# A block product inside a fast block product: seven smaller products for one, in fifteen of sixteen stages of an expert network

## The chip, the cores and the metric

The kernel runs on one core of a Trainium2 chip. A core has TensorE (matrix products, in the profile PE for the products and PEld for loading their stationary operand), VectorE (DVE), ScalarE (ACT), GpSimd (POOL), which here mostly issues gathers and scatters, and SyncE (SP), which issues most other transfers. Each takes its instructions in order. On-chip memory is SBUF, 128 partitions; TensorE writes its sums into the eight banks of PSUM, from which VectorE and ScalarE read them. The metric is the device time in microseconds of one execution; a kernel's time is the median of several.

## The reference, cut to what matters

```python
styles = w @ (affine_w * gain).T + affine_b
y = einsum('blc,oc->blo', x * styles[:, None, :], weight) * dcoefs[:, None, :]
y = clip(y + bias, -256, 256)                       # (8, 512, 512): 4096 tokens of 512

scores = softmax(y.reshape(4096, 512) @ Wr)         # 8 experts
G, idx = top_k(scores.T, 1024)                      # each expert takes its 1024 best tokens
X_in = y.reshape(4096, 512)[idx]                    # (8, 1024, 512)
h = gelu(einsum('ekd,edh->ekh', X_in, W1) + b1)     # (8, 1024, 2048)
X_e = einsum('ekh,ehd->ekd', h, W2) + b2            # (8, 1024, 512)
out = x + zeros.at[idx].add(G[..., None] * X_e)
```

All is float32. The two products of the experts are nearly all of the arithmetic.

## The kernel before, in words

A first part, to about 165 us of the profile, computes y and the scores and chooses the first expert's tokens. Then come eight experts, each in two passes p over half of the 2048 hidden columns (the loop at lines 1205 to 1228). A pass is a hidden stage (the first product, 1024 tokens x 512 x 1024 hidden columns, with Gelu, into the tile H) and an output stage (the second, whose rows are scaled by the gain and added to the result in memory by GpSimd's scatter, line 1156). So there are 16 hidden and 16 output stages.

Each stage splits its matrices into 2x2 blocks and uses a fast block product (Winograd's form of Strassen's): seven block products for eight, paid for by sums of blocks. For the hidden stage the token blocks are called 11, 12, 21, 22 with sums s1 to s4 (`left_sums`, line 927), and the weight blocks (i, j) with sums t1 to t4 (`weight_sum_steps`, line 183). A stage has four units, one for each 128 columns of a block: `hidden_unit` (line 1031) and `out_unit` (line 1102). A unit is seven functions p1 to p7, one block product each (two matmuls of 128x512 in a hidden unit, four of 128x256 in an output unit):

- p1 starts bank a, p6, p5 and p3 add further products to it; after each, ScalarE reads the bank, either as a copy ("snap", lines 1059 and 1123) or as the last result.
- p2 uses bank b: token block 12 by weight block (1, 0). VectorE adds p1's copy (line 1072), and ScalarE's Gelu makes the first block of H.
- p7 and p4 share bank c; VectorE adds copies to it (lines 1087 and 1096).

PSUM has two banks a, one b, two c, two for transposes (`ps_t`) and one small. `in_turns` (line 999) interleaves a unit with the last two products, p3 and p4, of the one before. It also releases side work behind a unit's mark (the sum of p2): at the third unit of a hidden stage the four sums of second weights, at the third unit of an output stage those of the next first weights; in an expert's second pass `fetch` for the next expert at the first hidden unit and `prepare` at the first output unit.

`fetch` calls `indices` (line 834): VectorE builds a one-hot tile `oh` (line 849) and `val`, TensorE turns them into token indices (line 855), and `gather` (line 904) fetches 8 x 128 token rows by GpSimd (line 913) into row buffers, of which there are four, writes them back to memory by SP (line 917) and reads them in a layout for VectorE's transposes (line 919). `prepare` (line 946) transposes on VectorE (line 952) and forms s1 to s4. In the first hidden stage the side work is `route_others` (line 737), the choice of tokens for the other seven experts: a long exchange between VectorE and small products of TensorE, which ends in the first output stage.

What sets the order: in the first part, TensorE's instructions are held in the written order by `in_order` (line 77). The experts' products (`product`, line 1025) are not: they are placed by the scheduling layer from the order of the calls and the dependencies, and `tc.issue_after` keeps side work behind its mark. Tiles of one tag share buffers: a new one waits until the old one's readers are done. H has one buffer, as has every weight block.

SP's loads stand in order: `load_w1` for the next pass is called after the hidden stage, `load_w2` after the output stage (lines 1222 and 1228), each four transfers of 512 KB that wait for their blocks.

Of the kernel before, what the change touches and what calls it, by code (L numbers as in the profile page):

```python
# [20 lines left out]
P = 128  # L21
# [4 lines left out]
def tile_modulated_expert_choice_ffn(  # L26
# [76 lines left out]
    pk = const.tile([P, P], I32, name="pk")  # L103
    nc.gpsimd.iota(pk, pattern=[[0, P]], base=0, channel_multiplier=1)
    pm = const.tile([P, P], I32, name="pm")
    nc.gpsimd.iota(pm, pattern=[[1, P]], base=0, channel_multiplier=0)
    ek = const.tile([P, P], I32, name="ek")
    nc.vector.tensor_scalar(ek, pk, E - 1, None, op0=ALU.bitwise_and)
    em = const.tile([P, P], I32, name="em")
    nc.vector.tensor_scalar(em, pm, E - 1, None, op0=ALU.bitwise_and)  # L110
    same = const.tile([P, P], BF16, name="same")
    nc.vector.tensor_tensor(same, ek, em, ALU.is_equal)
    ahead = const.tile([P, P], BF16, name="ahead")
    nc.vector.tensor_tensor(ahead, pk, pm, ALU.is_lt)
    nc.vector.tensor_mul(ahead, ahead, same)
# [49 lines left out]
    QD = D // 2  # L165
    w1_blocks, w2_blocks = {}, {}
# [28 lines left out]
    def weight_sums(kind, blk, name):  # L195
        for _ in weight_sum_steps(kind, blk, name):
            pass

# [538 lines left out]
    def route_others():  # L737

        ST = rt.tile([P, 2, P], F32, tag="ST", name="ST")
# [15 lines left out]
        mark = rt.tile([P, 2, P], F32, tag="run", name="mark")  # L755
# [18 lines left out]
        def ranks(mask, name):  # L774

            run = rt.tile([P, 2, P], F32, tag="run", name=f"run_{name}")
# [12 lines left out]
            nc.vector.tensor_copy(off, ps)  # L789
            return run, off  # L790


        sel = rt.tile([P, 2, P], F32, name="sel")
# [3 lines left out]
        eq = rt.tile([P, 2, P], F32, name="eq")  # L797
# [22 lines left out]
        pos_i = rt.tile([P, NT, E], I32, tag="ST", name="pos_i")  # L820
        nc.vector.tensor_scalar(pos_i.rearrange("p t e -> p (t e)"),
                                ps.rearrange("p h m -> p (h m)"), -1.0, None, op0=ALU.add)
        part = rt.tile([P, NT, E], I32, tag="part", name="part")
# [3 lines left out]
        part2 = rt.tile([P, NT, E], I32, tag="part", name="part2")  # L827
        nc.vector.tensor_scalar(part2, pos_i, 7, None, op0=ALU.logical_shift_right)
        hi = rt.tile([P, NT, E], BF16, name="hi")
        nc.vector.tensor_copy(hi, part2)  # L830
# [3 lines left out]
    def indices(e):  # L834
# [14 lines left out]
        nc.vector.tensor_tensor(  # L849
            oh, lo.unsqueeze(2).to_broadcast([P, NT, P]),  # L850
            iota_lo.unsqueeze(1).to_broadcast([P, NT, P]), ALU.is_equal,
        )
# [51 lines left out]
    def gather(e, i):  # L904
# [40 lines left out]

    def prepare(e):
# [9 lines left out]
        left_sums(xT[0, 0], xT[0, 1], xT[1, 0], xT[1, 1], s)  # L956

# [41 lines left out]
    def in_turns(units, between):  # L999
# [5 lines left out]
        for n in range(len(units)):  # L1005
# [15 lines left out]
            held = unit[5:]  # L1021
        for f in held:
            f()

    def product(ps, lefts, rights, start):
        n = len(lefts)
        for k in range(n):
            nc.tensor.matmul(ps, lefts[k], rights[k], start=(start and k == 0), stop=(k == n - 1),  # L1028
                             skip_group_check=True)

    def hidden_unit(e, p, u, H, early=False):
# [12 lines left out]

        def begin(cols):
# [11 lines left out]
        def snap(n):  # L1057
            t = sp.tile([P, HALF], F32, tag=f"snap{n}", name=f"snap{n}_{name}")
# [41 lines left out]
        return (begin, unit) if early else unit  # L1100

    def out_unit(e, p, v, H, b2_sb):
# [7 lines left out]
             for n in ("s1", "s2", "s3", "s4")}  # L1110
# [94 lines left out]
    for e in range(E):  # L1205
        b2_sb = fx.tile([P, D], F32, tag="b2", name=f"b2_{e}")
        nc.sync.dma_start(b2_sb, b2[e, :].partition_broadcast(P))
        for p in range(NP):
# [60 lines left out]
```

## Time and profile before

| | us |
|---|---|
| median of three runs | 1750.95 (1750.62 to 1751.68) |
| the profiled execution's own time | 1745.7 |
| its span, first to last instruction | 1743.9 |
| TensorE products busy | 1718.0 (99% of the span) |
| weight loads busy | 1136.2 (65%) |
| VectorE busy | 830.8 (48%) |
| ScalarE busy | 480.2 (28%) |
| granted TensorE clock, mean | 0.996 |

A row of instructions names line and engine, what is written from what, shape, and count. A float32 matmul stands as two passes, each with its own weight load, so a hidden unit's block product shows as x4 and an output unit's as x8. Matmul passes overlap in the pipeline: the time that counts is from the start of one to the start of the next. Tiles are named ps_a_h, ps_b_h, ps_c_h for the banks in a hidden stage, ps_a_o and so on in an output stage, hs_o for the sums of H's blocks, xs for those of the tokens, w_t for those of the weights, snap for ScalarE's copies.

### The profile page before, as it was taken

To read this page: it belongs to the slowest core of one execution; us is meant where nothing else is said; L and a number is where in the kernel's file an instruction comes from. 1 tells how busy PE (TensorE), PEld (TensorE's weight loads), DVE (VectorE), ACT (ScalarE), POOL (GpSimd) and SP (SyncE) were. 2 spreads that over 40 slices of the span, in tenths; PEclk is the share of its full clock that TensorE was granted. 3 is DMA by queue.
4 is the path that set the end of the run, shared out by engine and by line. 5 is a ranking of instruction groups with operands and counts; after the bars stand their busy time and mean duration, and the time that the engine had idled before them with its cause. 6 is when DMAs were issued, how large, how long until landed. Compare 5 with 4: busy or idle time off the path is not lost.

```text
span 1743.9 us, 17415 instructions
## 1 busy us (share of the span) xinstructions
PE 1718.0 (99%) x6646; PEld 1136.2 (65%) x6646; DVE 830.8 (48%) x1467; ACT 480.2 (28%) x845; POOL 293.5 (17%) x238
## 2 busy tenths in 40 slices
PE   9998999999999999999999999999999999999997
PEld 5775475665748485766758485766758484756656
DVE  5885884524535254624535254614444254614341
ACT  3543312223131322222231313222231313222231
POOL 0112013020212013110312012110302012110202
PEclk9999999999999999999999999999999999999999
DMA  9625527441574237442574237432564137332403
GB/s 207 171 50 197 192 55 179 106 85 49 97 201 73 48 61 183 90 85 55 100 191 85 49 63 176 90 79 55 112 179 90 46 64 186 75 79 61 85 0 49
DMA packets 143252, 178.59 MB, mean 102 GB/s; under 512 B 16825, under 2 KB 92857, under 8 KB 143041
## 3 DMA queue, kind: packets, MB, share of 16 engines
q1 hardware_dynamic: 118240, 115.19, 24.4%
q0 software_dynamic: 24912, 62.27, 21.0%
q8 instruction: 52, 0.85, 0.2%
q14 instruction: 32, 0.25, 0.0%
q10 hardware_dynamic: 16, 0.02, 0.0%
HBM read 120.46 MB, written 65.37 MB: 107 GB/s over the span
## 4 chain that ended last, share of the span: by engine, by line
PE 93%; DVE 4%; ACT 1%; issue 1%; DMA 1%; POOL 0%; POOLq 0%; DVEq 0%; ACTq 0%
PE ps_a_o L1028 25%; PE ps_a_h L1028 23%; PE ps_c_o L1028 12%; PE ps_c_h L1028 12%; PE ps_b_o L1028 6%; PE ps_b_h L1028 6%; PE ps_ya L81 2%; PE ps_yc L81 1%; DVE oh L849 1%; PE ps_y L81 1%; ACT xmT L500 1%; DVE mark L760 1%; PE ps_yt L727 1%; PE ps_a_h_a L1028 0%; PE ps_yb L81 0%
## 5 line engine op out<-in xcount | busy, mean ns | idle before, releaser
L1156 POOL DMA_INDIRECT out<-o_o,idx x128 | 213.2, 1666 | 1246.7 <-DVE o_o L1153 497.0
L1028 PE MATMUL ps_a_o<-w_t,hs_o 128*128 128x256 f32 x1024 | 243.3, 380 | 1.2
L1028 PE MATMUL ps_a_h<-xs,w_t 128*128 128x512 f32 x496 | 233.4, 592 | 0.0
L1028 PEld LDWEIGHTS ps_a_o<-w_t,hs_o 128*128 128x128 f32 x1024 | 192.3, 190 | 33.7 <-issue 7.2
L1028 PEld LDWEIGHTS ps_a_h<-xs,w_t 128*128 128x128 f32 x496 | 94.1, 190 | 119.1 <-issue 118.5
L1059 ACT COPY snap_h<-ps_a_h 128x512 f32<-128x512 f32 x186 | 108.2, 582 | 230.0 <-PE ps_a_h L1028 227.0
L1123 ACT ACTIVATE snap_o<-ps_a_o,gain 128x256 f32<-128x256 f32 x128 | 60.6, 474 | 346.7 <-PE ps_a_o L1028 346.7
L1087 DVE TENSOR_TENSOR snap_h<-snap_h,ps_c_h 128x512 f32<-128x512 f32 x64 | 43.9, 687 | 217.5 <-ACT snap_h L1059 217.5
L1072 DVE TENSOR_TENSOR ps_b_h<-ps_b_h,snap_h 128x512 f32<-128x512 f32 x62 | 43.4, 699 | 202.6 <-PE ps_b_h L1028 202.6
L1028 PE MATMUL ps_c_o<-w,hs_o 128*128 128x256 f32 x512 | 124.2, 380 | 0.0
L1028 PE MATMUL ps_a_o<-w,H 128*128 128x256 f32 x512 | 124.0, 379 | 0.0
L1028 PE MATMUL ps_a_o<-w,hs_o 128*128 128x256 f32 x512 | 121.6, 380 | 0.0
L1028 PE MATMUL ps_b_o<-w,H 128*128 128x256 f32 x512 | 121.1, 379 | 0.0
L1028 PE MATMUL ps_a_h<-xT,w 128*128 128x512 f32 x248 | 120.7, 594 | 0.0
L1028 PE MATMUL ps_c_h<-xs,w 128*128 128x512 f32 x256 | 120.5, 593 | 0.0
L1028 PE MATMUL ps_c_h<-xT,w_t 128*128 128x512 f32 x256 | 120.5, 593 | 0.0
L1028 PE MATMUL ps_c_o<-w_t,H 128*128 128x256 f32 x504 | 119.1, 379 | 0.0
L1028 PE MATMUL ps_a_h<-xs,w 128*128 128x512 f32 x248 | 118.2, 599 | 0.0
L1028 PE MATMUL ps_b_h<-xT,w 128*128 128x512 f32 x248 | 116.8, 593 | 0.0
L1028 PEld LDWEIGHTS ps_a_o<-w,H 128*128 128x128 f32 x512 | 97.1, 190 | 27.0 <-issue 15.5
L1028 PEld LDWEIGHTS ps_a_o<-w,hs_o 128*128 128x128 f32 x512 | 95.9, 190 | 21.8 <-ACT snap_o L1123 9.2
L1028 PEld LDWEIGHTS ps_c_o<-w,hs_o 128*128 128x128 f32 x512 | 97.0, 190 | 13.9 <-issue 0.6
(277 smaller groups left out, 1983.8 us busy)
## 6 DMA issues: line engine op xcount, KB each, us to landing
w<-in_w SPq DMA_DIRECT2D x120, 512.0 KB, 4.1
rows<-row SPq DMA_DIRECT2D x56, 260.0 KB, 3.9
xg<-rows SPq DMA_DIRECT2D x56, 256.0 KB, 6.4
x<-in_x SPq DMA_DIRECT2D x28, 256.0 KB, 8.4
y_dram<-ytok SPq DMA_DIRECT2D x5, 1024.0 KB, 4.3
w<-in_w SPq DMA_DIRECT2D x32, 128.0 KB, 3.5
y_dram<-ytok POOLq DMA_DIRECT2D x12, 256.0 KB, 5.0
b<-in_b SPq DMA_DIRECT2D x8, 256.0 KB, 4.2
```

The lines of the kernel that those rows point to most:

```text
L81: behind[engine] = make()
L500: nc.scalar.mul(t, t, styles[1][:, j, b : b + 1])
L727: nc.tensor.transpose(ps[:, o * P : (o + 1) * P], yT[:, o, t * P : (t + 1) * P], ident)
L760: nc.vector.tensor_scalar(mark, ST, cand[:, c + 1 : c + 2].bitcast(F32), None, op0=ALU.is_ge, op1=ALU.add, accum_out=cnt[:, c : c + 1])
L849: nc.vector.tensor_tensor(oh, lo.unsqueeze(2).to_broadcast([P, NT, P]), iota_lo.unsqueeze(1).to_broadcast([P, NT, P]), ALU.is_equal,)
L1028: nc.tensor.matmul(ps, lefts[k], rights[k], start=(start and k == 0), stop=(k == n - 1), skip_group_check=True)
L1059: nc.scalar.copy(t, st["a"])
L1072: added = nc.vector.tensor_add(st["b"], st["b"], st["s1"])
L1087: nc.vector.tensor_add(st["u4"], st["u4"], st["c"])
L1123: nc.scalar.mul(t, st["a"], scale)
L1156: nc.gpsimd.indirect_dma_start(out=last_rows[g] if e == E - 1 else out_rows, out_offset=bass.IndirectOffsetOnAxis(ap=idx[:, e, g : g + 1], ...
```

## The change: what it does

In 15 of the 16 hidden stages (all but the first) the product p2, block 12 by block (1, 0), over all four units, is itself done by the same seven-product form on its own 2x2 blocks: two groups r of seven products, each a single matmul of 128x256 (`second_level`). Its parts go to a tile q in SBUF; the banks are b and the two of `ps_t`. `hidden_stage` takes the place of `in_turns` there: units in the order 0, 2, 1, 3, the small products put behind the large ones by a plan, and `finish(u)` takes unit u's share of q to the sum with p1's copy and the Gelu. The sums that this needs are `second_sums` (tokens) and the four additions in `weight_sums`. An output stage's last p3 and p4 are handed on (`keep`, `held`) and issued inside the next hidden stage, and the second weights' load is called there, behind them (`then`).

To make room in SBUF: the first constants are in a pool that is given back; routing works in the buffers of gathered rows, whose number goes from four to three; the output units' sum s1 overwrites H's block; the token sums of the second level use the place of block 21. The copy of p1 has three buffers instead of two. The one-hot tile is built in four parts.

Left out of the diff below are the renamed routing tiles, the constants' pool, and lines that only hand on arguments.

```diff
 def weight_sums(kind, blk, name):
...
+        if kind == "w1":
+            b = {(k, j): blk[1, 0][:, k, j * Q : (j + 1) * Q] for k in range(2) for j in range(2)}
+            t = wpool.tile([P, 3, Q], F32, tag="w1_l2", name=f"w1_l2_{name}")
+            t1, t2, t4 = [t[:, n, :] for n in range(3)]
+            nc.vector.tensor_add(t1, b[0, 0], b[0, 1])
+            nc.vector.tensor_add(t2, t1, b[1, 1])
+            nc.vector.tensor_add(t4, t2, b[1, 0])
+            nc.vector.tensor_add(b[0, 1], b[0, 1], b[1, 1])
+            blk["l2"] = {**b, "t1": t1, "t2": t2, "t3": b[0, 1], "t4": t4}
...
-        nc.vector.tensor_tensor(
-            oh, lo.unsqueeze(2).to_broadcast([P, NT, P]),
-            iota_lo.unsqueeze(1).to_broadcast([P, NT, P]), ALU.is_equal,
-        )
+        for n in range(4):
+            here = slice(n * NT // 4, (n + 1) * NT // 4)
+            nc.vector.tensor_tensor(
+                oh[:, here, :], lo[:, here].unsqueeze(2).to_broadcast([P, NT // 4, P]),
+                iota_lo.unsqueeze(1).to_broadcast([P, NT // 4, P]), ALU.is_equal,
+            )
...
-            to = gp.tile([P, YW], F32, tag="row", name=f"row_{e}_{g}", bufs=4)
+            to = gp.tile([P, YW], F32, tag="row", name=f"row_{e}_{g}", bufs=3)
...
+    def second_sums(e):
+        s = tokens[e][0]
+        a = {(i, k): s["12"][:, k, i * Q : (i + 1) * Q] for i in range(2) for k in range(2)}
+        t = fx.tile([P, 4, Q], F32, tag="xT10", name=f"x2_{e}")
+        s2 = {f"s{n + 1}": t[:, n, :] for n in range(4)}
+        left_sums(a[0, 0], a[0, 1], a[1, 0], a[1, 1], s2)
+        tokens[e][0]["l2"] = {**s2, "11": a[0, 0], "12": a[0, 1], "22": a[1, 1]}
...
         left_sums(xT[0, 0], xT[0, 1], xT[1, 0], xT[1, 1], s)
+        second_sums(e)
...
+    def second_level(e, p, r):
+        s, blk = tokens[e][0]["l2"], w1_blocks[e, p]["l2"]
+        name = f"{e}_{p}_{r}"
+        q = sp.tile([P, 2, HALF], F32, tag="q", name=f"q_{name}", bufs=1)
+        out = {(i, j): q[:, j, i * Q : (i + 1) * Q] for i in range(2) for j in range(2)}
+        st = {}
+        def mm(tag, left, right, start):
+            if start:
+                st[tag] = (bank("b", f"q{name}", 1) if tag == "b" else
+                           ps_t.tile([P, HALF], F32, tag="t", name=f"ps_q{tag}_{name}"))[:, 0:Q]
+            product(st[tag], [blk[right][:, r * P : (r + 1) * P]], [s[left]], start)
+        def snap(n, scale=1.0):
+            t = sp.tile([P, Q], F32, tag=f"q{n}", name=f"q{n}_{name}", bufs=1)
+            nc.scalar.mul(t, st["a"], scale)
+            return t
+        def p1():
+            mm("a", "11", (0, 0), True)
+            st["s1"] = snap(1)
+        def p2():
+            mm("b", "12", (1, 0), True)
+            return nc.vector.tensor_add(out[0, 0], st["b"], st["s1"])
+        def p6():
+            mm("a", "s2", "t2", False)
+            st["u2"] = snap(2)
+        def p7():
+            mm("c", "s3", "t3", True)
+        def p5():
+            mm("a", "s1", "t1", False)
+            st["u4"] = snap(4, -1.0)
+            nc.vector.tensor_sub(out[1, 1], st["u4"], st["c"])
+        def p3():
+            mm("a", "s4", (1, 1), False)
+            nc.scalar.mul(out[0, 1], st["a"], -1.0)
+        def p4():
+            mm("c", "22", "t4", False)
+            nc.vector.tensor_add(out[1, 0], st["c"], st["u2"])
+        return [p1, p2, p6, p7, p5, p3, p4], q
+
+    def hidden_stage(e, p, H, between, held, then):
+        unit = {u: hidden_unit(e, p, u, H) for u in range(U)}
+        steps, results = zip(*[second_level(e, p, r) for r in range(2)])
+        g = [iter(x) for x in steps]
+        def finish(u):
+            return unit[u][1](results[u % 2][:, u // 2, :])
+        def second(r, n=1):
+            for _ in range(n):
+                done = next(g[r])()
+            return done
+        mark = None
+        plan = [
+            (0, [partial(second, 0)], [partial(second, 0)], [partial(second, 0)], [partial(second, 0)],
+             [partial(second, 0)], []),
+            (2, [], [partial(second, 0)], [partial(second, 0), partial(finish, 0), partial(finish, 2)],
+             [partial(second, 1)], [partial(second, 1)], [partial(second, 1)]),
+            (1, [partial(second, 1)], [partial(second, 1)], [], [partial(second, 1)],
+             [partial(second, 1), partial(finish, 1)], []),
+            (3, [partial(finish, 3)], [], [], [], [], []),
+        ]
+        for n, (u, *fill) in enumerate(plan):
+            p1, _, p6, p7, p5, p3, p4 = unit[u]
+            for f, behind_it in zip((p1, held[0], p6, held[1], p7, p5), fill):
+                f()
+                if n == 0 and f is held[1]:
+                    then()
+                for step in behind_it:
+                    mark = step() or mark
+            for work in between.get(n, ()):
+                with tc.issue_after(mark.ins):
+                    work()
+            held = [p3, p4]
+        for f in held:
+            f()
...
-        def p2():
-            if not early:
-                st["b"] = bank("b", name, 1)
-                mm(st["b"], "12", (1, 0), True)
-            added = nc.vector.tensor_add(st["b"], st["b"], st["s1"])
-            nc.scalar.activation(out[0, 0], st["b"], AF.Gelu, bias=bias[0])
+        def p2(other=None):
+            to = st["s1"] if other is not None else st["b"]
+            added = nc.vector.tensor_add(to, st["b"] if other is None else other, st["s1"])
+            nc.scalar.activation(out[0, 0], to, AF.Gelu, bias=bias[0])
             return added
...
         s = {n: sp.tile([P, U, P], F32, tag=f"h{n}", name=f"h{n}_{name}")
-             for n in ("s1", "s2", "s3", "s4")}
+             for n in ("s2", "s3", "s4")}
+        s["s1"] = a[1, 0]
         left_sums(a[0, 0], a[0, 1], a[1, 0], a[1, 1], s)
...
-            units = [partial(hidden_unit, e, p, u, H) for u in range(U)]
             if e == p == 0:
+                units = [partial(hidden_unit, e, p, u, H) for u in range(U)]
                 units[0:2] = [lambda unit=unit: unit for _, unit in early]
-            in_turns(units, work)
+                in_turns(units, work)
+            else:
+                hidden_stage(e, p, H, work, held, partial(load_w2, e, p))
...
+            if e == p == 0:
+                work[0] = [partial(second_sums, 0)]
-            in_turns([partial(out_unit, e, p, v, H, b2_sb) for v in range(GH)], work)
-            if nxt[0] < E:
-                load_w2(*nxt)
+            held = in_turns([partial(out_unit, e, p, v, H, b2_sb) for v in range(GH)], work,
+                            keep=nxt[0] < E)
```

More of the change, by code (lines that the diff above doesn't have):

```diff
@@ L102, in tile_modulated_expert_choice_ffn @@
     NL = P // E
[L103 to L110, printed above, removed]
     same = const.tile([P, P], BF16, name="same")
-    nc.vector.tensor_tensor(same, ek, em, ALU.is_equal)
     ahead = const.tile([P, P], BF16, name="ahead")
-    nc.vector.tensor_tensor(ahead, pk, pm, ALU.is_lt)
-    nc.vector.tensor_mul(ahead, ahead, same)
+    with tc.tile_pool(name="init", bufs=1) as init:
+        pk = init.tile([P, P], I32, name="pk")
+        nc.gpsimd.iota(pk, pattern=[[0, P]], base=0, channel_multiplier=1)
+        pm = init.tile([P, P], I32, name="pm")
+        nc.gpsimd.iota(pm, pattern=[[1, P]], base=0, channel_multiplier=0)
+        ek = init.tile([P, P], I32, name="ek")
+        nc.vector.tensor_scalar(ek, pk, E - 1, None, op0=ALU.bitwise_and)
+        em = init.tile([P, P], I32, name="em")
+        nc.vector.tensor_scalar(em, pm, E - 1, None, op0=ALU.bitwise_and)
+        nc.vector.tensor_tensor(same, ek, em, ALU.is_equal)
+        nc.vector.tensor_tensor(ahead, pk, pm, ALU.is_lt)
+        nc.vector.tensor_mul(ahead, ahead, same)
     iota_lo = const.tile([P, P], BF16, name="iota_lo")
@@ L165, in tile_modulated_expert_choice_ffn @@
     QD = D // 2
+    Q = HALF // 2
     w1_blocks, w2_blocks = {}, {}
@@ L737, in route_others @@
     def route_others():
-        ST = rt.tile([P, 2, P], F32, tag="ST", name="ST")
+        spare = [gp.tile([P, YW], F32, tag="row", name=f"spare{n}", bufs=3) for n in range(3)]
+        ST, run_, sel, eq, part_ = [
+            spare[n // 2][:, n % 2 * 2 * P : (n % 2 + 1) * 2 * P].rearrange("p (h t) -> p h t", t=P)
+            for n in range(5)]
         ps = ps_t.tile([P, 2, P], F32, tag="t", name="ps_ST")
@@ L751, in total @@
             return ps
-        mark = rt.tile([P, 2, P], F32, tag="run", name="mark")
+        mark = run_
         cand = two_bits[:, 0, :]
@@ L774, in ranks @@
         def ranks(mask, name):
-            run = rt.tile([P, 2, P], F32, tag="run", name=f"run_{name}")
+            run = run_
             nc.vector.tensor_tensor_scan(run.rearrange("p h t -> p (h t)"),
@@ L790, in ranks @@
             return run, off
-        sel = rt.tile([P, 2, P], F32, name="sel")
         cnt = rt2.tile([P, 1], BF16, tag="cnt", name="cnt_gt")
@@ L796, in route_others @@
         tot = total(cnt, "gt")
-        eq = rt.tile([P, 2, P], F32, name="eq")
         nc.vector.tensor_scalar(eq, ST, thr, None, op0=ALU.is_equal)
@@ L818, in route_others @@
             nc.tensor.transpose(ps[:, h, :], pos[:, h, :], ident)
-        pos_i = rt.tile([P, NT, E], I32, tag="ST", name="pos_i")
+        pos_i, part = [t.bitcast(I32).rearrange("p h t -> p (h t)").rearrange("p (t e) -> p t e", e=E)
+                       for t in (ST, part_)]
         nc.vector.tensor_scalar(pos_i.rearrange("p t e -> p (t e)"),
                                 ps.rearrange("p h m -> p (h m)"), -1.0, None, op0=ALU.add)
-        part = rt.tile([P, NT, E], I32, tag="part", name="part")
         nc.vector.tensor_scalar(part, pos_i, P - 1, None, op0=ALU.bitwise_and)
@@ L826, in route_others @@
         nc.vector.tensor_copy(lo, part)
-        part2 = rt.tile([P, NT, E], I32, tag="part", name="part2")
-        nc.vector.tensor_scalar(part2, pos_i, 7, None, op0=ALU.logical_shift_right)
+        nc.vector.tensor_scalar(part, pos_i, 7, None, op0=ALU.logical_shift_right)
         hi = rt.tile([P, NT, E], BF16, name="hi")
-        nc.vector.tensor_copy(hi, part2)
+        nc.vector.tensor_copy(hi, part)
         for e in range(1, E):
@@ L997, in bank, with in_turns @@
         return ps_mm.tile([P, HALF], F32, tag=tag, name=f"ps_{tag}_{name}", bufs=bufs)
-    def in_turns(units, between):
+    def in_turns(units, between, keep=False):
         held = []
@@ L1021, in in_turns @@
             held = unit[5:]
+        if keep:
+            return held
         for f in held:
@@ L1043, in mm, with second_product @@
                     [s[left][:, k, :] for k in range(2)], start)
+        def second_product():
+            st["b"] = bank("b", name, 1)
+            mm(st["b"], "12", (1, 0), True)
+            return p2()
         def begin(cols):
@@ L1057, in snap @@
         def snap(n):
-            t = sp.tile([P, HALF], F32, tag=f"snap{n}", name=f"snap{n}_{name}")
+            t = sp.tile([P, HALF], F32, tag=f"snap{n}", name=f"snap{n}_{name}",
+                        bufs=3 if n == 1 else 2)
             nc.scalar.copy(t, st["a"])
@@ L1099, in hidden_unit @@
         unit = [p1, p2, p6, p7, p5, p3, p4]
-        return (begin, unit) if early else unit
+        if early:
+            return begin, unit
+        if e == p == 0:
+            unit[1] = second_product
+        return unit
     def out_unit(e, p, v, H, b2_sb):
@@ L1225, in tile_modulated_expert_choice_ffn @@
                 work[0] = [partial(prepare, e + 1)]
-            in_turns([partial(out_unit, e, p, v, H, b2_sb) for v in range(GH)], work)
-            if nxt[0] < E:
-                load_w2(*nxt)
+            if e == p == 0:
+                work[0] = [partial(second_sums, 0)]
+            held = in_turns([partial(out_unit, e, p, v, H, b2_sb) for v in range(GH)], work,
+                            keep=nxt[0] < E)
 def kernel(**inputs):
```

## The prediction

> **What bounds the kernel now.** I read the page's busy table and its clock row first, then the chain that ended last, then the chain in order of time for one expert.
>
> ```profile
> PE 1718.0 (99%) x6646; PEld 1136.2 (65%) x6646; DVE 830.8 (48%) x1467; ACT 480.2 (28%) x845; POOL 293.5 (17%) x238
> ...
> PEclk9999999999999999999999999999999999999999
> ...
> PE 93%; DVE 4%; ACT 1%; issue 1%; DMA 1%; POOL 0%; POOLq 0%; DVEq 0%; ACTq 0%
> ```
>
> TensorE is busy all the time, at a granted clock of 0.996, and it is 93% of the chain. What counts is how far apart its passes start, not how long one is said to take. The chain in order of time, for the end of one hidden stage and the start of its output stage (start, length, what):
>
> ```profile
> 597.35 5.15 PE ps_a_h L1028 x12
> 602.50 1.72 PE ps_b_h L1028 x4
> ...
> 618.10 0.86 PE ps_c_o L1028 x4
> 619.04 1.97 PE ps_a_o L1028 x8
> 621.01 0.86 PE ps_c_o L1028 x4
> 621.87 5.18 PE ps_a_o L1028 x24
> ```
>
> Each fp32 matmul is two passes. Twelve passes of 512 columns take 5.15 us, 0.429 each; 24 passes of 256 columns take 5.18 us, 0.216 each. The rows' mean durations (592 and 380 ns) contain the overlap and are not used. A hidden stage is 112 passes of 512, 48.07 us; an output stage is 224 of 256, 48.34 us: 96.4 together, and an expert has two. An expert's period (573.31 to 768.23, the same row of two experts) is 194.9 us, so only 2.1 us are anything else: the index products (0.82 us with 0.2 before them, below) and at each output stage three short waits, of 0.10, 0.24 and 0.08 us. The timeline (start, length, what) shows the 0.24: four passes from 617.94 are through at 618.80, and the next product starts at 619.04.
>
> ```profile
> 617.94 1.03 PE L1028 MATMUL ps_c_o<-w,hs_o 128*128 128x256 f32 x4
> 619.04 1.97 PE L1028 MATMUL ps_a_o<-w_t,hs_o 128*128 128x256 f32 x8
> ...
> 618.22 0.68 DVE L931 SCALAR_TENSOR_TENSOR hs_o<-hs_o,H 128x512 f32<-128x512 f32 x1
> ...
> 671.77 1.02 PE L1028 MATMUL ps_a_h<-xT,w 128*128 128x512 f32 x2
> 672.83 0.97 PE L855 MATMUL ps_idx<-val,oh 128*128 128x16 bf16 x32
> ...
> 667.83 4.42 DVE L849 TENSOR_TENSOR oh<-lo,iota_lo 128x4096 bf16<-128x4096 bf16 x1
> ```
>
> VectorE's L931 (the sum s2 of the first output unit) ends at 618.90, 0.14 before the product that uses it. The one-hot tile of L849 is what holds the index products.
>
> **The change part by part.**
>
> *Products (TensorE, on the path).* In 15 of 16 hidden stages the product p2 goes: 4 units x 2 matmuls x 2 passes = 16 passes of 512, 6.867 us. In its place come 2 halves x 7 products x 2 passes = 28 passes of 256, 6.042 us. Gain 0.825 us a stage, **12.4 us** in all. The step rests on a lone pair of 256-column passes between 512-column ones costing what it costs in a row. The trace has such borders: 47 steps from a 512-pass to a 256-pass lie a median 429 ns apart, and 46 the other way 216. The weight load, 190 ns, hides under either. Here a rule of the Trainium skill speaks against the change: TensorE: Matmul & The Clock Gate, section "Back-to-back issue gap", says that in a stream of weight load and matmul pairs the spacing is set by both, measured at 81 ns for 128 columns and 131 for 512. A straight line through these gives 98 at 256, 0.75 of a 512-pass instead of a half. By that estimate 28 x 0.75 x 0.429 = 9.0 us against 6.87: 2.1 us lost a stage, 32 us in all, 1783 us. The row decides: 0.216 is 0.503 of 0.429. I take 12.4.
>
> *New waits among those products.* The built order gives TensorE, from a hidden stage's start (us, at the steps above): unit 0's p1 to 1.72, small p1 to 2.15, the last output unit's p3 to 3.9, small p2 to 4.3, p6 to 6.0, small p6 to 6.5, that unit's p4 to 8.2, small p7 to 8.6, p7 to 10.3, small p5 to 10.8, p5 to 12.5, then unit 2's p1 to 14.2, unit 0's p3 to 15.9, small p3 to 16.3, unit 2's p6. Every product that adds to a bank which ScalarE copied has at least 1.7 us between; a copy lands about 0.95 us after the pass that it reads ends (0.59 and the step either side, 0.10 late at 611.81 where 0.86 us lay between). The small bank's turns have 3.9 us or more. The tightest place: unit 2's p6 at 16.3 needs a ScalarE copy that stands behind unit 0's Gelu, which waits for a VectorE sum: 12.5 + 0.2 + 0.59 + 0.69 + 0.72 and two steps of 0.05 give 14.8, the copy ends at 15.4. 0.9 us to spare. Later, the Gelu of rebuilt unit 1 waits for VectorE, and behind it on ScalarE stands the copy that unit 1's p3 needs; in the built order VectorE does this sum ahead of the four weight sums (1.22 each), which leaves 0.7 us. So I cost these waits at **0**; bounds 0 and 0.5 us a stage (7.5 in all), no gain being possible here. I add 0.5 us in all for margins this thin.
>
> *VectorE and ScalarE work (hidden).* A stage gains on VectorE 4 weight sums of 128x256 (0.42 each, as L787's row), 6 sums (0.48, as L1134), and half of 4 token sums: 5.4 us; the four finish sums (0.69) replace four of L1072 (0.70). Stretches by stage show it at 14.1 to 27.8 us busy of 48 to 49. ScalarE gets 8 of 0.47, 3.8 us, on 17.2 of 48. What hides them is TensorE's stage itself; where cover is thinnest, the output stage with the four transposes, the next expert's sums delay the third output unit's s2 from 731.6 to about 733, needed at about 740.4.
>
> *Start of the output stage.* The order changes: all of p7 now comes before p6, 0.86 us more cover, while VectorE does both units' s3 first, so s2 is the fourth sum, not the third (0.60 later). It ends 4.14 us after the last hidden pass, plus 0.14 is 4.28, and the product is due at 4.32. The 0.24 goes, and the 0.08 after it, since the products it split are gone. s1 is now written over H's third block, which no product reads; the built waits of that sum name VectorE alone. Gain 0.32 x 15 = **4.8 us**; bounds 0 (s2 as late as now) and 4.8.
>
> *Index products.* They wait for the one-hot tile of L849, now in four parts, two of which let VectorE's output sums pass. From the small p2, which releases this work, TensorE has 8.2 us of products ahead of them (6.0 before); VectorE needs about 8.1 for all its queue. The 0.2 goes: 7 x 0.2 = **1.4 us**; bounds 0 and 1.4.
>
> *First output stage.* The token sums of expert 0 (4 x 0.42) and one more s-sum now stand inside the routing chain on VectorE, while TensorE reaches the off_eq, off_sel and ps_pos products earlier by 0.86, 0.43 and about 0. Walked through, TensorE waits some 1.6 us there where it now waits 0.35. Cost **1.2 us**; bounds 0 and 2.5.
>
> *Loads.* Carrying p3 and p4 into the next stage moves the second-weight loads (4 x 512 KB, some 4.0 us to land) behind these products; they already waited for the same blocks (SP issued them over 649.53 to 662.88), and are first used 37 us into the stage. On SP, the first transposed gather now goes behind two more row writes, the second behind one first-weight load more, and it still stands ahead of those that wait longest. Row buffers go from 4 to 3: VectorE uses the gathers from 720.2 on, they are asked for at 687.6 and 700.7, 6.1 us to land; one more round of gather and write (about 9 us) fits. Cost 0; if the cover went, the transposes and the token sums would come late by the excess, and the output units' s-sums behind them. The scoped constants, shared routing tiles and a third copy buffer have no other price; the early loads' order and waits are unchanged.
>
> *Sum.* -12.4 - 4.8 - 1.4 + 1.2 + 0.5 = -16.9 us. The profiled execution took 1745.7 us with a span of 1743.9; its span becomes 1727.0. The median shown is 5.25 above the profiled run, and I carry that over: 1750.95 - 16.9 = **1734 us**.
>
> **Rivals.**
>
> *Only the passes.* Half or more of what the small waits promise doesn't come (their margins are 0.04 and 0.1 us), or new ones of some 0.3 us a stage arise: -12.4 + 1.2 + 0 to 7 gives 1740 to 1747. For it: thin margins in a built order that no trace shows yet. Against: those in the middle of a stage are 0.7 us and more.
>
> *The waits eat the gain.* Of 15 stages' fourteen small products, half expose 0.12 us each, as that one 512-copy does now: 0.83 us a stage, 12.4 us in all: 1748 to 1754, no change. Against it: they have 3.9 us of cover, where the exposed one has 0.86.
>
> *Slower: the borders.* A small product's weights must wait for a bank, so its 190 ns load no longer goes ahead, at 28 borders a stage. Break-even is the gain over the borders, 0.825 / 28 = 29 ns each without the other gains, 40 with them. At half the load, 95 ns: 2.7 us a stage, minus 1.1, times 15: 24 us slower, 1775; the skill's spacing above ends near it. For it: such alternation on every second product isn't in the trace. Against: its 93 borders at nothing, and in the output stages 256-passes that wait for banks at 0.216.
>
> **How the numbers follow.** This kernel's three runs span 0.06%; 0.2% (3.5 us) is about what a measurement can tell from no change. Forecast (1729 to 1739.5) 0.58, only the passes (to 1747) 0.20, no change 0.08, slower 0.14. Predicted 1734, the likeliest's own range 1729 to 1739.5. The range reaches over the second case and the upper bounds of the waits: 1728 to 1748. Faster 0.78, same 0.08, slower 0.14.
>
> **What would show it.** TensorE's small products 0.43 us apart from the next; a chain still some 93% TensorE; an expert's period near 192.4 us instead of 194.9; no step before the first output p6; VectorE near 910 us busy, ScalarE near 535. It is wrong if 256-column passes between 512-column ones lie more than 0.22 apart, if TensorE waits for ScalarE's copies or for the VectorE sums in mid-stage, or if the gathers come late and the output stage after a fetch grows.

## The result, and the profile after

The changed kernel takes **1732.3 us** (median of four runs, 1731.5 to 1733.0), the kernel before 1751.3 beside it: a ratio of 0.989, 95% interval 0.987 to 0.991. That is 19.0 us less; the forecast was 1734, 16.9 less. The page of the profiled execution (1732.0 us, span 1730.2), busy table, clock row and shares of the chain that ended last:

```profile
PE 1701.4 (98%) x6826; PEld 1171.7 (68%) x6826; DVE 895.3 (52%) x1670; ACT 516.1 (30%) x965; POOL 309.1 (18%) x238
...
PEclk9998999999999999999999999999999999999999
...
PE 94%; DVE 2%; ACT 1%; DMA 1%; issue 0%; another core or an unknown queue 0%; POOLq 0%; POOL 0%; SPq 0%; DVEq 0%; ACTq 0%
```

TensorE is still 94% of the chain (93% before). VectorE gained 64.5 us of work and ScalarE 35.9, and their shares of the chain did not grow (4% and 1% before). The chain in order of time (start, length, what): the small products, the end of one hidden stage with the start of its output stage, the index products, and the next expert's first row:

```profile
563.58 1.72 PE ps_a_h L1056 x4
...
596.24 0.43 PE ps_qa L1056 x2
596.67 1.72 PE ps_c_h L1056 x4
598.39 0.43 PE ps_qc L1056 x2
598.82 6.87 PE ps_a_h L1056 x16
...
616.13 1.73 PE ps_b_o L1056 x8
617.86 1.73 PE ps_c_o L1056 x8
619.59 6.96 PE ps_a_o L1056 x32
...
670.12 1.72 PE ps_a_h L1056 x4
671.83 0.79 PE ps_idx L869 x32
...
756.03 1.72 PE ps_a_h L1056 x4
```

A small product (two passes of 256 columns) takes 0.43, before and behind products of 512 columns. The output stage's p7 is now whole, eight passes in 1.73, and p6 follows at once: the 0.24 is gone. The index products follow without a step. The expert's period, 563.58 to 756.03, is 192.45 us; it was 194.9, and 192.4 was forecast.

The two profiles must not be subtracted from each other: 1745.7 and 1732.0 differ by 13.7 only. Stage by stage, the two agree to the first hidden stage within 1.3 us; then that stage, up to its output stage, takes 57.0 us in the profile before and 60.3 in the one after, and from the second hidden stage on the kernel after gains steadily. The 3.3 us are in the head, by which I mean everything ahead of the second hidden stage. Its first hidden stage takes 57.0 to 58.4 us or 60.3 to 62.7, and either kernel can have either (the experiments with the unchanged kernels). To be free of it, runs are compared below by **the rest**: from the second hidden stage's first pass to the end of the last pass, in us from each trace.

| kernel | first hidden stage | the rest | time of this execution |
|---|---|---|---|
| before (profile shown) | 57.0 | 1465.2 | 1745.7 |
| before again | 61.9 | 1465.2 | 1749.5 |
| before, s1 in place | 62.7 | 1461.3 | 1749.9 |
| before, s1 in place, one-hot in four | 57.0 | 1460.4 | 1740.7 |
| after with direct p2 | 61.8 | 1459.0 | 1746.2 |
| after, half the stages | 62.1 | 1452.4 | 1737.2 |
| after (profile shown) | 60.3 | 1446.6 | 1732.0 |
| after again | 57.0 | 1446.7 | 1727.5 |
| after, more VectorE work | 57.1 | 1446.7 | 1727.4 |
| after, small ones in a row | 57.0 | 1447.0 | 1726.5 |
| after, 128 columns | 58.4 | 1449.8 | 1733.1 |
| two products rebuilt | 57.0 | 1436.7 | 1717.3 |

The change takes 18.6 us from the rest. The experiments were run on two chips. On one the kernel before takes about 1751, and the four profiles from there have the long first hidden stage; on the other it takes about 1745, and the six profiles from there have the short one. Two profiles of one kernel (before and before again, after and after again) differ in the head alone: their rests agree within 0.1 us.

### The profile page after: what moved, and what is told of

Same layout as the page of the kernel before. It is cut to its first block, busy times and chain, and to the rows that moved or that the text cites. A ratio compares the mean times of both kernels' runs of the same rounds, so it can differ in the third digit from the quotient of the medians.

```text
span 1730.2 us, 18022 instructions
## 1 busy us (share of the span) xinstructions
PE 1701.4 (98%) x6826; PEld 1171.7 (68%) x6826; DVE 895.3 (52%) x1670; ACT 516.1 (30%) x965; POOL 309.1 (18%) x238
## 4 chain that ended last, share of the span: by engine, by line
PE 94%; DVE 2%; ACT 1%; DMA 1%; issue 0%; another core or an unknown queue 0%; POOLq 0%; POOL 0%; SPq 0%; DVEq 0%; ACTq 0%
PE ps_a_o L1056 25%; PE ps_a_h L1056 25%; PE ps_c_o L1056 13%; PE ps_c_h L1056 12%; PE ps_b_o L1056 6%; PE ps_qa L1056 3%; PE ps_ya L81 2%; PE ps_qc L1056 1%; PE ps_yc L81 1%; PE ps_y L81 1%; PE ps_b_q L1056 1%; ACT xmT L512 1%; DVE spare L775 1%; PE ps_yt L739 1%; PE ps_a_h_a L1056 0%; PE ps_yb L81 0%
## 5 line engine op out<-in xcount | busy, mean ns | idle before, releaser
L1286 POOL DMA_INDIRECT out<-o_o,idx x128 | 229.2, 1791 | 1188.3 <-DVE o_o L1283 434.1
L1056 PE MATMUL ps_a_o<-w_t,hs_o 128*128 128x256 f32 x512 | 121.8, 381 | 0.0
L1056 PE MATMUL ps_a_o<-w_t,H 128*128 128x256 f32 x512 | 121.4, 379 | 0.0
L1056 PE MATMUL ps_a_h<-xT,w 128*128 128x512 f32 x248 | 117.1, 594 | 0.0
L1056 PEld LDWEIGHTS ps_a_o<-w_t,hs_o 128*128 128x128 f32 x512 | 96.0, 190 | 15.3 <-issue 2.9
L1056 PEld LDWEIGHTS ps_b_o<-w,H 128*128 128x128 f32 x512 | 97.2, 190 | 13.2
L1056 PEld LDWEIGHTS ps_a_o<-w_t,H 128*128 128x128 f32 x512 | 96.4, 190 | 14.4 <-issue 0.5
```

Source lines behind the costliest of these rows:

```text
L1286: nc.gpsimd.indirect_dma_start(out=last_rows[g] if e == E - 1 else out_rows, out_offset=bass.IndirectOffsetOnAxis(ap=idx[:, e, g : g + 1], ...
```

## The experiments

**The kernel before, again.**

> The kernel before, unchanged, for a second profile of its head. The profile that I predicted from took 5.25 us less than its kernel's median, and I carried that gap over. Theory: the gap is a few us in the head (before the second hidden stage, which started at 269.6 us there), which most executions have: here that stage starts at 272 to 275 us and the time is about 1750, with an expert's period of 194.9 as before. Rival: the gap lies around the span or along the stages: the stage starts at 269.6 again, or the period is longer than 194.9.

Measured: 1749.47 us; the rest is 1465.2, as before to 0.02 us, and the second hidden stage starts at 273.3. VectorE's and then TensorE's timeline of this run at that place (start, length, what, and in brackets the idle time before it and what ended it):

```profile
171.96 0.76 DVE L986 COPY xT<-ps_xg 128x256 f32<-128x256 f32 x2 [3.60 <-remote]
...
172.44 1.22 PE L81 MATMUL ps_a_h_a<-xT,w 128*128 128x128 f32 x4 [3.42 <-DVE xT L986]
```

TensorE stands 3.4 us for a copy of VectorE's that waits for something the profile can't name. The profile before lacks this step. The second hidden stage starts 3.7 us later here than there, and that is most of the gap of 5.25 us between that profile and its kernel's median. The step is in the kernel before, so it is not the change's.

**The second level undone.** Diff against the kernel after:

```diff
+    def two_levels(e, p):
+        return False
...
-                hidden_stage(e, p, H, work, held, partial(load_w2, e, p))
+                if two_levels(e, p):
+                    hidden_stage(e, p, H, work, held, partial(load_w2, e, p))
+                else:
+                    in_turns([partial(hidden_unit, e, p, u, H) for u in range(U)], work,
+                             held=held, then=partial(load_w2, e, p))
```

(Not shown: `hidden_unit` uses the direct `second_product` everywhere, the second-level sums are left out, and `in_turns` takes the carried products.)

> The kernel after with its second level undone: p2 is again one direct product of two 512-column matmuls in all stages, and the second-level sums are gone; p3 and p4 are still carried into the next stage, s1 is still in place, the one-hot tile in four parts. Theory: only the passes come back, 15 x 0.825 = 12.4 us: 1744.7, an expert's period of 194.0 against 192.4. Rival 'the order of the products does it' (fewer waits in the rebuilt stages carry a good part of the gain): 1748 to 1751. Rival 'the order alone is enough': 1732 to 1736.

Measured: 1745.14 us (ratio to before 0.9966, 0.9955 to 0.9978), 12.8 over the kernel after; in the rest 1458.97 against 1446.58, **12.39 us**, to the 12.4 forecast. The short steps between passes, beyond 0.429 and 0.216, add up to the same in both traces within 0.1 us: this part of the gain is the passes, and nothing else is in it. Everything else of the change, without the second level, is worth 6.2 us in the rest.

**Half of it.**

```diff
+    def two_levels(e, p):
+        return p == 1
```

(The rest of the diff is as in the run above, but the tokens' second-level sums stay.)

> The kernel after with the second level only in the second hidden stage of each expert (8 of the 15 stages keep it, 7 have the direct p2). Theory: each stage that loses it costs 0.825 us whatever its neighbours do: 7 x 0.825 = 5.8 us over the kernel after, 1738.1, and exactly 7/15 of what undoing all of it costs. Rival, that the gain is in the borders or the waits of neighbouring stages: not in proportion, more than 2 us off that share.

Measured: 1737.97 us; the rest is 5.78 us over the kernel after's, and 7/15 of 12.39 is 5.78. Each stage has its own price, and neighbours don't enter.

**One edit on the kernel before: s1 in place.**

```diff
-             for n in ("s1", "s2", "s3", "s4")}
+             for n in ("s2", "s3", "s4")}
+        s["s1"] = a[1, 0]
```

> The kernel before with one edit alone: the output unit's sum s1 is written over the block of H that it comes from, so the tile for it is gone. Its built order puts the whole of p7 before p6 at the output stages' start. Theory: this edit by itself is the 4.8 us that I put down to the start of the output stage: the 0.24 and 0.08 us waits are gone in the trace, 1751.3 - 4.8 = 1746.5. Rival, that these waits went because the second level moved the products around: no change, 1751.

Measured: 1746.95 us (ratio to before 0.9981, 0.9971 to 0.9990); the rest is 3.9 us shorter. TensorE's timeline of this run, the start of an output stage:

```profile
623.59 1.89 PE L1028 MATMUL ps_b_o<-w,H 128*128 128x256 f32 x8
625.32 1.89 PE L1028 MATMUL ps_c_o<-w,hs_o 128*128 128x256 f32 x8
627.05 1.95 PE L1028 MATMUL ps_a_o<-w_t,hs_o 128*128 128x256 f32 x8
628.83 1.03 PE L1028 MATMUL ps_a_o<-w,H 128*128 128x256 f32 x4
```

p7 is in one piece and p6 starts 1.73 after it starts: the 0.24 went with this edit alone, as the theory said. But from p6 to the next product is 1.78, not 1.73: 0.06 of the old 0.08 stayed, between p6's first and second pass. So 3.9, not 4.8. The edit looks like a saving of memory; the built order after it has the sums and products of the output stage's start in other places.

**And the one-hot tile in four parts.** The diff is the loop over `n` in `indices`, shown with the change.

> The kernel before with two edits: s1 in place, and the one-hot tile in four parts; no second level, nothing carried. Theory: the 0.2 us step before the index products goes from the trace with the four parts alone, 7 x 0.2 = 1.4 us less than with s1 in place only: an expert's period of 194.2 against 194.4. Rival: that step goes only when the carried products and the small ones put more work ahead of the index products (8.2 us against 6.0): it stays at 0.1 to 0.2.

Measured: 1740.72 us for one run; the rest is 0.9 us shorter than with s1 alone, a period of 194.3. TensorE's timeline of this run around the index products:

```profile
668.55 1.88 PE L1030 MATMUL ps_a_h<-xs,w_t 128*128 128x512 f32 x4
670.27 0.75 PE L857 MATMUL ps_idx<-val,oh 128*128 128x16 bf16 x24
670.88 1.10 PE L1030 MATMUL ps_a_h<-xT,w 128*128 128x512 f32 x2
671.82 0.35 PE L857 MATMUL ps_idx<-val,oh 128*128 128x16 bf16 x8
672.03 1.10 PE L1030 MATMUL ps_a_h<-xT,w 128*128 128x512 f32 x2
```

The wait is gone (670.27 follows 668.55 by four passes), but the last eight index products now stand apart, and two 512-column passes after an index product take 0.94 instead of 0.86. Such a border costs 0.08, once more per expert, so that 0.13 of 0.2 is gained. In the kernel after, and in the kernel with direct p2, where the last output products are carried ahead of them, the index products are in one piece and the whole 0.2 is won. The theory held for the wait and missed the border.

**Where the weight load begins to cost.**

```diff
-            product(st[tag], [blk[right][:, r * P : (r + 1) * P]], [s[left]], start)
+            for c in range(0, Q, P):
+                product(st[tag][:, c : c + P], [blk[right][:, r * P : (r + 1) * P]],
+                        [s[left][:, c : c + P]], start and c == 0)
```

> The kernel after with every small product's 256 columns done as two passes of 128, with the same weights: the same columns in twice the passes, 56 more-or-less 128-column passes a stage in place of 28 of 256. It asks where the weight load, 190 ns in the profile, stops being hidden. If passes are spaced by columns alone: 0.108 each, no change, 1732. Theory: a pass can't start faster than its weights load, 0.190 each: 56 x 0.082 = 4.6 us a stage, 15 stages 69 us: 1801. By the spacing for 128 columns that the Trainium skill gives (TensorE: Matmul & The Clock Gate, Back-to-back issue gap: 81 against 131 ns, 0.62 of a 512-column pass, 0.266 here): 133 us, 1865.

Measured: 1733.14 us for one run; the rest is 3.1 us over the kernel after's. The theory had 69, and the estimate from the skill's page 133: both are refuted. TensorE's timeline, then the weight loads' of the same stretch:

```profile
577.92 0.61 PE L1056 MATMUL ps_qa<-x,w 128*128 128x128 f32 x4
578.37 1.88 PE L1056 MATMUL ps_a_h<-xs,w_t 128*128 128x512 f32 x4
...
577.50 0.19 PEld L1056 LDWEIGHTS ps_qa<-x,w 128*128 128x128 f32 x1 [0.24 <-issue]
577.93 0.41 PEld L1056 LDWEIGHTS ps_qa<-x,w 128*128 128x128 f32 x3 [0.24 <-issue]
```

Four passes of 128 columns take 0.45, 0.111 each, and each has its own load: three loads, each recorded as 0.19 long, are through in 0.41. 840 passes of 0.111 in place of 420 of 0.216 are some 2.7 us more, about what is seen. The 190 ns of the row are how long a load is recorded as under way, not how far apart loads must be.

**More VectorE work at the thinnest place.**

```diff
         def finish(u):
+            if u == 1:
+                for _ in range(4):
+                    t = results[1][:, 0, :]
+                    nc.vector.tensor_tensor(t, t, t, ALU.max)
```

> The kernel after with four more VectorE operations of 128x512 (the maximum of the rebuilt block with itself, so no value changes) ahead of unit 1's finishing sum in each of the 15 stages: 4 x 0.61 = 2.4 us a stage, 37 us of VectorE in all, at the place where I counted 0.7 us to spare. If the order on ScalarE stood as it was, unit 1's Gelu and the copy behind it would be 2.4 us late, and p3 would wait 1.7 us a stage, 25 us: 1757. Theory: the scheduler puts the copy ahead of that Gelu, as the built order shows, and VectorE's work stays hidden: 1731 to 1735. If it costs 1757, my margin was real and the order does not save it.

Measured: 1727.16 us, ratio to before 0.9894 (0.9878 to 0.9911), the kernel after's own; the rest is the same to 0.1 us. VectorE's busy time went up by 37.7 us to 933.0 at no cost. ScalarE's timeline of this run:

```profile
596.09 0.59 ACT L1189 COPY snap_h<-ps_a_h 128x512 f32<-128x512 f32 x1 [2.88 <-PE ps_a_h L1056]
...
598.93 0.72 ACT L1202 ACTIVATE H<-snap_h,b_sb 128x512 f32<-128x512 f32 x1
```

and of the profile after:

```profile
600.05 0.72 ACT L1198 ACTIVATE H<-snap_h,b_sb 128x512 f32<-128x512 f32 x1 [2.35 <-DVE snap_h L1197]
600.68 0.56 ACT L1185 COPY snap_h<-ps_a_h 128x512 f32<-128x512 f32 x1
```

The copy that p3 needs now stands well before the Gelu of the delayed sum, where the kernel after has it behind. The margin that I counted as 0.7 us was 0.85 (in the kernel after the copy ends at 601.24, p3 starts at 602.09), but it is not a limit: with the added work in the program, the scheduler built the two the other way round.

**The small products in a row.** The plan asks for all seven of a half behind one product of a unit:

```diff
-            (0, [partial(second, 0)], [partial(second, 0)], [partial(second, 0)], [partial(second, 0)],
-             [partial(second, 0)], []),
...
+            (0, [partial(second, 0, 7)], [], [], [], [], []),
```

(The second half's seven are asked for in the same way, behind one product of the next unit.)

> The kernel after with the seven small products of each half asked for in a row behind one product of a unit, not one behind each; what then stands between them is what the scheduler puts there (in the built order two of the small ones, or one and half of an output product: 0.86 us). The waits measured so far: a product that adds to a bank of 512 columns copied by ScalarE is 0.08 to 0.10 late with 0.86 us of cover. A copy of 256 columns is 0.2 us shorter (0.38 against 0.58). Theory: 0.86 is then just enough, no new steps at the small products, an expert's period of 192.4 to 192.6. Rival: with so little cover each of some six adding products a stage is 0.1 late, 0.6 us a stage: a period near 193.6, 9 us over the kernel after on the same chip.

Measured: 1726.50 us, one run; the rest is 0.3 us longer, a period of 192.5. One step of 0.31 us stands in the whole trace that the kernel after lacks. The chain in order of time of this run, small products one after another:

```profile
578.27 0.43 PE ps_qa L1056 x2
578.70 0.43 PE ps_b_q L1056 x2
579.13 0.43 PE ps_qc L1056 x2
579.56 0.43 PE ps_qa L1056 x2
```

Between small p1 and small p6, which adds to the bank that ScalarE copies after p1, there are two other small products, 0.86 us, and p6 is on time. The plan written by hand is not what hides the small copies: in the order that the scheduler builds, 0.86 us or so lies ahead of the products that wait for them.

**The kernel after, again.**

> The kernel after, unchanged, on the same chip as the run above, for the head. The six profiles so far have the first hidden stage, up to its output stage, at 57.0 to 57.1 us (before, and three runs of another day's chip where the kernel before takes 1745) or at 58.4 to 62.7 (the others, where it takes 1751). Theory: the kernel after has either head, as the kernel before has; its period is 192.45 again whatever the head does, and its time is 1726 with the short head and 1732 with the long one. Rival, that the long head belongs to the change: the head is long here whatever the kernel before takes.

Measured: 1727.52 us, with 57.0 us for the first hidden stage. The same copy of VectorE's in VectorE's timeline of this run, and then of the profile after:

```profile
170.15 0.76 DVE L1011 COPY xT<-ps_xg 128x256 f32<-128x256 f32 x2 [0.20 <-PE ps_xg L81]
```

```profile
174.44 0.75 DVE L1011 COPY xT<-ps_xg 128x256 f32<-128x256 f32 x2 [3.52 <-remote]
```

One kernel, two heads, and the rest equal to 0.1 us: the long head does not belong to the change.

**A second product rebuilt.** As the price of a rebuilt product held in every test, p3 was given the same treatment. The core of the diff:

```diff
+            for n, key in ((2, (1, 0)), (3, (1, 1))):
+                b = {(k, j): blk[key][:, k, j * Q : (j + 1) * Q] for k in range(2) for j in range(2)}
...
-            nc.vector.tensor_add(st["u4"], st["u4"], st["c"])
-            nc.scalar.activation(out[1, 1], st["u4"], AF.Gelu, bias=bias[1], scale=-1.0)
+            nc.vector.tensor_add(out[1, 1], st["u4"], st["c"])
+            nc.scalar.activation(out[1, 1], out[1, 1], AF.Gelu, bias=bias[1], scale=-1.0)
...
+            if rebuilt:
+                nc.vector.tensor_add(out[0, 1], out[0, 1], st["u4"])
+                nc.scalar.activation(out[0, 1], out[0, 1], AF.Gelu, bias=bias[1], scale=-1.0)
```

The small products of p3 write straight into H's block, block s4 of the tokens gets sums of its own, with s1 in place, and the small copies share the output units' buffers.

> The kernel after with a second of the seven products, p3, rebuilt in the same way in the 15 stages: 14 more small products a stage for four units' p3 (seven for two units at a time), 16 passes of 512 less and 28 of 256 more; p3 no longer adds to a bank, its sum with u4 is made by VectorE over the block of H that it goes to. Unit 1's p4 is held until after unit 3's p5. Theory: the price of a rebuilt product is that of its passes again, 15 x 0.825 = 12.4 us: 1720, an expert's period near 190.8. Rival: fourteen more small products a stage crowd the copies, and the output stage's start waits again for the sum s2 (up to 0.4 us a stage): 1721 to 1726. Rival: VectorE (some 1000 us busy) or ScalarE becomes the bound in the hidden stage: 1732 or more.

Measured: **1717.82 us**, ratio to before 0.9841 (0.9825 to 0.9858), on the chip where the kernel after takes 1727.5: the fastest of all. The rest is 10.0 us shorter than the kernel after's, where 12.4 was the theory: a fifth of the gain is lost, as the first rival had it, but its cause is only partly the one that it named. The plan of the products is another too, so what the loss consists of is read from the steps in the trace. Its busy row, and TensorE's timeline at one of the places:

```profile
PE 1690.8 (99%) x7006; PEld 1205.2 (70%) x7006; DVE 994.9 (58%) x1912; ACT 558.5 (33%) x1085; POOL 312.0 (18%) x238
```

```profile
584.11 1.88 PE L1060 MATMUL ps_a_h<-xT,w 128*128 128x512 f32 x4
585.82 0.60 PE L1060 MATMUL ps_qa<-x,w 128*128 128x256 f32 x2
586.25 0.59 PE L1060 MATMUL ps_qc<-xT,w_l 128*128 128x256 f32 x2
586.68 1.96 PE L1060 MATMUL ps_a_h<-xs,w_t 128*128 128x512 f32 x4
588.48 0.59 PE L1060 MATMUL ps_qa<-xs,w 128*128 128x256 f32 x2
```

p1 ends at 585.82, and p6 adds to the bank that ScalarE has to copy first. The direct p3 used to stand between; now only two small products do, 0.86 us, and p6's four passes take 1.80 instead of 1.72. There are 30 such steps of 0.08 in this trace; the kernel after has 15, of 0.13. That is 0.5 us more in all. The larger part is elsewhere: the index products now stand in four pieces, 28 returns to float32 passes where there were 7, 1.8 us. Together that is 2.3 of the 2.4 us that are missing. The output stage's start does not wait for s2 any more than in the kernel after, and nothing shows VectorE, at 995 us, as the bound.

## Why the prediction was right, point by point

The terms against the runs, all in us over the whole kernel. The second column is the term, the third what the rest shows, or the sum of the steps between passes beyond 0.429 and 0.216:

| step | forecast | measured |
|---|---|---|
| passes of the rebuilt product | -12.4 | -12.39 |
| start of the output stage | -4.8 | -3.9 |
| last output products, at the start of the hidden stage | none | -0.8 |
| index products | -1.4 | -1.5 |
| first output stage | +1.2 | +0.04 (in the head) |
| thin margins | +0.5 | 0 |
| sum | -16.9 | -18.6 (in the rest) |
| carried from profile to median | +5.25 | 3.7 of it seen in the head |

*Passes.* The step from the row to the forecast was right, and by its own mechanism: undoing the second level costs what the passes cost. In the trace after, 212 steps from a 512-column pass to a 256-column one are a median 429 ns apart and 211 the other way 216, as the 93 borders before were. The spacing that I took from the Trainium skill (TensorE: Matmul & The Clock Gate, "Back-to-back issue gap") would have made it slower, 1783 by my estimate; for these float32 passes the measurement decides, here also at 128 columns, where that spacing gives 0.62 of a 512-column pass and the run 0.26. The rival of the borders was refuted with its cause: even 128-column passes, too short to hide a load of 190 ns, are 0.111 apart.

*Start of the output stage.* The steps from p7 to p6 were 3.65 us in the trace before (15 of 0.24) and are none after; the 0.08 inside p6 was 1.1 and is 0.8. My sentence that "the 0.08 after it" goes "since the products it split are gone" was wrong: 0.06 remains in all 15 stages, between p6's first and second pass. So the term is 3.9, which the edit of s1 brings by itself. The tightest margin of the forecast, 0.04 us, held for p6's first pass; the second is the one that comes late.

*What I had not seen.* In the trace before, the last output unit's p3, which stands near each hidden stage's start, has a step of 0.03 between its first two passes, and once waits 0.2: 0.8 us in all. It is gone wherever these products are carried, in the kernel after and in the one with direct p2, and stays where they are not. It made up for the 0.9 that the output stage's start fell short: that the sum came so near is in part luck.

*Index products.* 1.49 us of wait before, none after. The one-hot tile's parts alone leave a border of 0.08, as the run with them showed. The kernel with direct p2 has them in one piece as well, so carried products and parts together are enough, without the small products. Whether the longer cover alone would do, with the tile in one part, no run tests; and the kernel with two rebuilt products has four pieces, so more work ahead is not the whole rule.

*First output stage.* Wrong. I had TensorE wait 1.6 us for the routing chain; the stage takes 45.26 us, and took 45.22. The product off_eq comes 11.7 us into the stage (12.5 before), so it does come 0.8 earlier as I had it, yet TensorE waits only 0.15 for it and 0.15 for off_sel. VectorE's timeline of the profile after shows why:

```profile
237.72 0.41 DVE L943 TENSOR_TENSOR x<-xT 128x256 f32<-128x256 f32 x1
...
238.12 0.41 DVE L944 TENSOR_TENSOR x<-xT 128x256 f32<-128x256 f32 x1
...
240.17 0.40 DVE L945 SCALAR_TENSOR_TENSOR x<-x,xT 128x256 f32<-128x256 f32 x1
240.48 0.16 DVE L798 CAST ends_eq<-spare 128x2 bf16<-128x2 f32 x1
240.55 0.68 DVE L943 TENSOR_TENSOR hs_o<-H 128x512 f32<-128x512 f32 x1
```

Three of the four token sums do stand ahead of the tile that off_eq needs, as I had them. But the output units' sums, 0.68 each, gave way: 11 of them stood there in this stage before, 8 after. There my walk was wrong.

*Thin margins.* No new step is in the trace, and none from late loads or gathers. The 0.86 us of cover that I named as too short is so in every kernel here (0.08 to 0.13 late each time), and the small products don't meet it, since a copy of 256 columns takes 0.38 against 0.58. The rival "the waits eat the gain" is what the kernel with two rebuilt products shows at 15 more places, at 0.08 a step. (Its 12.4 us on a forecast of 1734 give 1746; the 1748 to 1754 that I wrote don't follow from it.) The rival "only the passes" fell with the 6.2 us that the change without its second level brings.

*What I carried over.* The sum was made against a profile with the short head and carried to a median with the long one. I had no reason for it on record but the gap itself. It held, because the kernel after had the long head too: its profile, 1732.0, starts the second hidden stage as late as the one of the kernel before at 1749.5 does, to 1.0 us. The two errors of 1.2 and 0.5 make up the 1.7 by which the kernel came out below the forecast.

VectorE was forecast near 910 us and ScalarE near 535; they are at 895 and 516. For the small sums and copies I took 0.48 and 0.47 each from other rows; they take 0.42 and 0.38.

## What to carry to other kernels

Where TensorE is the bound, price a change of products by the start-to-start distance of its passes, not by recorded durations, and then price each consumer of a bank by its cover: here 0.86 us is some 0.1 too little for a 512-column copy and enough for a 256-column one. When a profile's own time is off its kernel's median, find the place before comparing two profiles; comparing one stretch behind it settled terms of 1 us that the times, with a spread of 2 to 4 us, could not. And look at the built order after each small edit: giving up one tile moved the products of every output stage.

## What the runs showed of the hardware

- Float32 passes are 0.429, 0.216 and 0.111 us apart at 512, 256 and 128 columns: about 0.83 ns a column and a few ns a pass. The weight load recorded beside each as 190 ns long doesn't set a floor; loads follow one another by 0.11. The Trainium skill (TensorE: Matmul & The Clock Gate, "Architectural detail: the array is 16× 32×32, not 1× 128×128") has a reason: a matmul can begin before its load completes. The trace agrees as far as its records go: of the four 128-column passes shown, the second starts at 578.03, and its load is recorded from 577.93 to 578.12. That this is the cause of the spacing no run shows.
- Going back from the bf16 index products to 512-column float32 passes costs 0.08 us each time, between the first and the second pass.
- A product that waited shows a further step in the same place: 0.075 us in p6 behind the wait of 0.24 in the kernel before, and 0.055 in the kernel after, where p6's first pass is on time (619.42, the next at 619.70 instead of 619.64). So a product can start on time and still come late, one pass further on.
- The head has two lengths, mostly by a stall of some 3.5 us in which VectorE and ScalarE both stand idle and the profile names no one; five of the twelve profiles have it. A 16 KB instruction packet on a DMA queue ends 0.5 to 1.1 us before they go on in these five, but the seven without the stall have that packet too. What it is stays open; nothing was tried on it.
